# Seven 128x128 block products for P4 as well in layer 1, with stores issued ahead of loads

## The chip, the cores and the metric

The kernel runs on one core of one Trainium2 chip. The metric is the device time of one execution in microseconds (us), the median of several. A single execution of one core has a state of fast or unknown; every profiled run used here was fast, at a mean granted TensorE clock of 0.998 or 0.999 over its span. TensorE is called PE, the VectorE DVE, the ScalarE ACT, the GpSimd POOL, and SyncE SP, as in the profile.

## The reference

There are 128 graphs of 128 nodes with 512 features, and two layers of attention with 8 heads over an adjacency matrix. Everything is f32.

```python
# layer 0                                     # layer 1, on the output of layer 0
Q, K, V = x @ W_q + b_q, ...                  q, k, v = x @ Wq.T + bq, ...
scores = Q K^T / 8 + a_i + c_j + b_g          logits = q k^T / 8
       + log(adj + 1e-9)                             + log(clip(adj, 1e-8))
out = softmax(scores) V + x                   out = (softmax(logits) v) @ Wo.T + bo
                                              return layer_norm(x + out) * gamma + beta
```

Each layer has 512x512 weight matrices (three in layer 0, four in layer 1), and they take most of PE's time.

## The kernel before

Graphs are handled in groups of four: groups 0 to 31 are layer 0, groups 32 to 63 layer 1. One "matrix" is one weight applied to one group: v, q, k, and in layer 1 also o, the output matrix, which lags one group behind. There are 64 x 3 + 31 = 223 of them; the last group's output is computed plainly. The exponential of the log of the adjacency is a multiplication, so the softmax is `exp(scores) * adj`, divided by its sum, and the sum comes out of the mixing by a column of ones in v.

Each matrix is multiplied by Strassen's scheme, in the form with few additions: seven products P1 to P7 of 256x256 quarters in place of eight. A table of slots says which product stands where; "b" belongs to the matrix before. One of the seven, P2, is itself done by seven products of 128x128 blocks, in four phases "P2.1" to "P2.4" between which DVE combines what stands in PSUM:

```python
    SLOTS = ("P1", "P2.1"), ("P4 b",), ("P3 b", "P2.2"), ("P6", "P2.3"), ("P5",), ("P7", "P2.4"), ()
    PHASES = {"1": ("P1", "P2", "P5"), "2": ("P6",), "3": ("P7",), "4": ("P4", "P3")}
```

Every matmul is issued as two of 64 columns each, which run side by side on PE:

```python
        for half in HALVES:                     # columns 0 to 63, then 64 to 127
            nc.tensor.matmul(dst[half], lhsT[:, half], rhs, start=start, stop=stop, ...)
```

The rest of a group hangs on these slots: `pre` runs before a slot's products, `post` after them.

```python
            put(pre, a + 4 + step * k, scores, t, k)           # two graphs at a time, k = 0, 1
            put(pre, a + 7 + step * k, mix, t, (2 * k, 2 * k + 1))
            put(post, a + 7 + step * k, normalise, t, k)
            put(post, a + 8 + step * k, move, t, k, ...)       # o -> aT, transposed by 16 transfers
            ...
            put(post, first + (-1 if t == 0 else 2 + 7 * (b // 2) * late), load_graph, n, b, nc.sync)
            put(post, first + (11, 16 if t == NG + 1 else 13)[late], load_adjacency, n, nc.sync)
            ...
                    put(post, o + stored, store, t, k)         # h -> out, on the same queue (SP)
```

`move` transposes the attention's output into the buffer aT by sixteen transfers of 32 rows; the first eight fill columns 0 to 63 of every graph, the last eight columns 64 to 127:

```python
        for i in range(Q):
            for q in range(Q):
                src = v[i * S : (i + 1) * S, :, q // 2, (q % 2) * S : (q % 2 + 1) * S]
                engines[(i * Q + q) % len(engines)].dma_start(d[q * S : (q + 1) * S, :, i], src)
```

## Time and profile before

| | before |
|---|---|
| time, median of 3 runs (lowest to highest) | 3219.67 us (3216.62 to 3220.31) |
| profiled run | 3217.19 us, span 3215.3 us |
| busy over the span: PE, DVE, POOL | 99%, 62%, 57% |
| one group of layer 1 (scores to scores) | 55.56 us, some up to 56.7 |
| chain that ended last | PE 93%, SP's queue 3%, DMA 1% |

PE carries the time, but 3% of the chain runs through the queue that issues loads and stores. This is PE's timeline of the kernel before, in a layer 1 group (columns: start us, length us, engine, line, what, out<-in, rows and columns of the weight tile, size, count):

```profile
2231.44 1.90 PE L128 MATMUL p0o<-wo,T_o 128*64 128x256 f32 x16
2233.17 1.90 PE L128 MATMUL p2o<-wo,aT 128*64 128x256 f32 x16
2234.89 0.39 PE L128 MATMUL p1v<-wv1i,inner 128*64 128x128 f32 x4
2235.11 1.90 PE L128 MATMUL p3v<-wv,T 128*64 128x256 f32 x16
...
2237.16 2.06 PE L128 MATMUL s<-qT,kT 64*128 64x128 f32 x32
```

Products follow each other at their pitch. Between the block products of v and P3 of o (`p2o<-wo,aT`, 16 records) stands P4 of o (`p0o<-wo,T_o`), 1.73 us of work. The mixing isn't here: it ended at 2229.06.

### The profile page before, as it was taken

To read this page: it belongs to the slowest core of one execution; us is meant where nothing else is said; L and a number is where in the kernel's file an instruction comes from. 1 tells how busy PE (TensorE), PEld (TensorE's weight loads), DVE (VectorE), ACT (ScalarE), POOL (GpSimd) and SP (SyncE) were. 2 spreads that over 40 slices of the span, in tenths; PEclk is the share of its full clock that TensorE was granted. 3 is DMA by queue.
4 is the path that set the end of the run, shared out by engine and by line. 5 is a ranking of instruction groups with operands and counts; after the bars stand their busy time and mean duration, and the time that the engine had idled before them with its cause. 6 is when DMAs were issued, how large, how long until landed. Compare 5 with 4: busy or idle time off the path is not lost.

```text
span 3215.3 us, 95438 instructions
## 1 busy us (share of the span) xinstructions
PE 3192.1 (99%) x39970; PEld 2371.2 (74%) x39970; DVE 1988.4 (62%) x4075; ACT 1132.9 (35%) x1949; POOL 1826.5 (57%) x1892
## 2 busy tenths in 40 slices
PE   9999999999999999999999999999999999999998
PEld 6777777777777777777777777777777777777775
DVE  6666666666666666675565555555565555555565
ACT  2333333333333333333333333333333333333332
POOL 4434433434433434475766767676766767676775
PEclk9999999999999999999999999999999999999999
DMA  5333333333333333342434334343433334343432
GB/s 126 84 80 83 78 83 70 83 80 84 79 84 67 84 82 83 92 112 55 93 72 78 89 75 94 72 98 67 91 75 77 89 75 95 72 99 66 90 75 76
DMA packets 1017246, 265.83 MB, mean 83 GB/s; under 512 B 942704, under 2 KB 949872, under 8 KB 1016816
## 3 DMA queue, kind: packets, MB, share of 16 engines
q1 hardware_dynamic: 1015728, 258.39, 36.0%
q8 instruction: 319, 5.23, 0.7%
q10 hardware_dynamic: 832, 1.05, 0.1%
q14 instruction: 111, 0.91, 0.1%
q0 software_dynamic: 256, 0.26, 0.0%
HBM read 159.92 MB, written 67.11 MB: 71 GB/s over the span
## 4 chain that ended last, share of the span: by engine, by line
PE 93%; SPq 3%; DMA 1%; POOL 1%; DVE 1%; issue 1%; ACT 0%; DVEq 0%; POOLq 0%; ACTq 0%
PE p3v L128 10%; PE p0q L128 9%; PE p3k L128 9%; PE s L128 8%; PE av L128 7%; PE p2v L128 7%; PE p2q L128 7%; PE p2k L128 6%; PE p0o L128 6%; PE p0k L128 4%; PE p3q L128 4%; PE p0v L128 3%; SPq L128 3%; PE p2o L128 3%; PE p1q L128 3%; PE p1v L128 3%
## 5 line engine op out<-in xcount | busy, mean ns | idle before, releaser
L128 POOL TENSOR_TENSOR xn<-o,xn 128x512 f32<-128x512 f32 x128 | 151.1, 1201 | 661.2 <-DVE o L128 423.3
L128 DVE TENSOR_TENSOR e<-e,adjT 128x1024 f32<-128x1024 f32 x256 | 419.0, 1677 | 139.4 <-ACT e L128 139.4
L128 POOL TENSOR_TENSOR xn<-xn,row 128x512 f32<-128x512 f32 x256 | 361.7, 1435 | 169.9 <-DVE gw L128 138.0
L128 PE MATMUL p0q<-T,wq 128*64 128x256 f32 x2256 | 267.5, 379 | 0.0
L128 PE MATMUL p3k<-T,wk 128*64 128x256 f32 x2256 | 267.5, 379 | 0.0
L128 PE MATMUL p3v<-wv,T 128*64 128x256 f32 x2256 | 267.4, 379 | 0.0
L128 PE MATMUL s<-qT,kT 64*128 64x128 f32 x4096 | 263.1, 278 | 0.0
L128 PE MATMUL av<-v,e 128*64 128x65 f32 x8192 | 262.0, 221 | 0.0
L128 PEld LDWEIGHTS av<-v,e 128*64 128x64 f32 x8192 | 257.8, 137 | 1.0 <-issue 0.8
L128 PEld LDWEIGHTS s<-qT,kT 64*128 64x128 f32 x4096 | 238.6, 188 | 22.6 <-issue 12.1
L128 POOL TENSOR_TENSOR h<-h,gamma 128x512 f32<-128x512 f32 x122 | 156.3, 1281 | 115.0 <-ACT h L128 115.0
L128 PEld LDWEIGHTS p3k<-T,wk 128*64 128x64 f32 x2256 | 159.5, 137 | 67.4
L128 PEld LDWEIGHTS p3v<-wv,T 128*64 128x64 f32 x2256 | 159.0, 137 | 67.6
L128 PEld LDWEIGHTS p0q<-T,wq 128*64 128x64 f32 x2256 | 159.4, 137 | 67.1
L128 POOL TENSOR_TENSOR T<-xT 128x512 f32<-128x512 f32 x128 | 193.9, 1515 | 18.0 <-DVE xT L128 14.4
L128 ACT COPY o<-av 128x520 f32<-128x520 f32 x256 | 151.8, 593 | 133.2 <-PE av L128 120.8
L128 POOL TENSOR_TENSOR h<-h,xn 128x512 f32<-128x512 f32 x124 | 157.7, 1303 | 43.2 <-ACT h L128 40.4
L128 DVE SCALAR_TENSOR_TENSOR gw<-xn,gw 128x512 f32<-128x512 f32 x256 | 177.4, 693 | 4.4
L128 DVE STREAM_TRANSPOSE xT<-xT 128x512 f32<-128x512 f32 x252 | 177.1, 703 | 0.7 <-issue 0.7
L128 PE MATMUL p0o<-wo,T_o 128*64 128x256 f32 x1488 | 176.6, 379 | 0.0
L128 DVE TENSOR_TENSOR t1q<-p1q,t1q 128x128 f32<-128x128 f32 x189 | 54.5, 288 | 180.2 <-PE p1q L128 180.2
L128 POOL TENSOR_TENSOR h<-h,beta 128x512 f32<-128x512 f32 x122 | 156.5, 1283 | 9.6
(231 smaller groups left out, 6559.1 us busy)
## 6 DMA issues: line engine op xcount, KB each, us to landing
x1d<-xn SPq DMA_DIRECT2D x64, 512.0 KB, 3.0
xT<-x1d SPq DMA_DIRECT2D x512, 64.0 KB, 2.5
xn<-x1d SPq DMA_DIRECT2D x64, 512.0 KB, 6.9
xT<-in_x_dram SPq DMA_DIRECT2D x496, 64.0 KB, 2.8
xn<-in_x_dram SPq DMA_DIRECT2D x62, 512.0 KB, 4.1
aT<-o SPq DMA_DIRECT2D x984, 32.0 KB, 2.0
out_dram<-h SPq DMA_DIRECT2D x60, 512.0 KB, 4.6
adjT<-in_adj_dram SPq DMA_DIRECT2D x256, 64.0 KB, 3.7
```

Of the source, the lines that this page charges most:

```text
L128: return lambda *args, **kw: self.tc.keep_in_program_order(f(*args, **kw))
```

## The change

P4 of the layer 1 matrices is done by seven 128x128 block products too, in phases "P4.1" to "P4.4" between the outer products. That removes one block product in eight. To pay for it in the other engines, counts and small sums go to POOL; loads are issued later, so that the stores of h stand ahead of them in SP's queue; the last group's operations are reordered. Because P4 leaves slot 1, the first scores and the first mixing of a layer 1 group move one slot later (`L * (1 - k)`).

```diff
-    SLOTS = ("P1", "P2.1"), ("P4 b",), ("P3 b", "P2.2"), ("P6", "P2.3"), ("P5",), ("P7", "P2.4"), ()
+    SLOTS = (
+        ("P1", "P4.1 b", "P2.1"), ("P4 b",), ("P3 b", "P4.2 b", "P2.2"), ("P6", "P4.3 b", "P2.3"), ("P5", "P4.4 b"),
+        ("P7", "P2.4"), (),
+    )
+    INSIDE = {t: ("P2", "P4") if t > NG else ("P2",) if t else () for t in range(LAST)}
+    INSIDE.update({("qk", NG): (), ("o", NG): ()})
+    INSIDE.update({("o", t): ("P2", "P4") if t > NG else () for t in range(NG, LAST)})
...
-    for i in range(4):
-        nc.tensor.matmul(busy[:, 0:N], ones, ones, start=True, stop=True)
+    for i in range(20):
+        nc.tensor.matmul(busy[0 : P // 2, 0 : P // 2], ones, ones, start=True, stop=True)
...
-            put(pre, a + 4 + step * k, scores, t, k)
+            put(pre, a + 4 + L * (1 - k) + step * k, scores, t, k)
...
-                put(pre, a + 7 + step * k, mix, t, (2 * k, 2 * k + 1))
-                put(post, a + 7 + step * k, normalise, t, k)
+                m = a + 7 + L * (1 - k) + step * k
+                put(pre, m, mix, t, (2 * k, 2 * k + 1))
+                put(post, m, normalise, t, k)
...
-                put(post, first + (-1 if t == 0 else 2 + 7 * (b // 2) * late), load_graph, n, b, nc.sync)
+                put(post, first + (-1 if t == 0 else 2 + (8 if t > NG + 1 else 11) * (b // 2) * late), load_graph, n, b, nc.sync)
-            put(post, first + (11, 16 if t == NG + 1 else 13)[late], load_adjacency, n, nc.sync)
+            put(post, first + (11, 16 if t == NG + 1 else 14)[late], load_adjacency, n, nc.sync)
+            if "P4" in INSIDE[n]:
+                put(post, first + (18, 24)[late], lambda n: inner_sums(TS[n], n, "P4"), n)
... (phases of P4 in inner(); counts on POOL; residual, statistics and scaling of h at other slots;
     weight sums of P4; the list of the last group in another order, stores on two queues)
```

## The prediction

> **What bounds the kernel now.** I began with the page's busy times and slices.
>
> ```profile
> span 3215.3 us, 95438 instructions
> PE 3192.1 (99%) x39970; PEld 2371.2 (74%) x39970; DVE 1988.4 (62%) x4075; ACT 1132.9 (35%) x1949; POOL 1826.5 (57%) x1892
> ...
> PE   9999999999999999999999999999999999999998
> ```
>
> TensorE (PE) is busy from start to end. But the ends of matmuls are modelled and neighbours overlap, so 99% may hide waits. I therefore read the pitch, start to start, from the timeline of PE in layer 1 (columns: start us, length us, what):
>
> ```profile
> 2200.84 0.39 PE L128 MATMUL p1q<-inner,wq 128*64 128x128 f32 x4
> 2201.05 0.39 PE L128 MATMUL p1q<-xT,wq1i 128*64 128x128 f32 x4
> 2201.27 1.90 PE L128 MATMUL p3k<-xT,wk 128*64 128x256 f32 x16
> 2203.00 0.61 PE L128 MATMUL p1k<-xT,wk 128*64 128x128 f32 x8
> 2203.44 0.39 PE L128 MATMUL p1k<-inner,wk1i 128*64 128x128 f32 x4
> 2203.65 1.90 PE L128 MATMUL p0q<-T,wq 128*64 128x256 f32 x16
> ```
>
> A whole outer product (16 records: 2 output blocks x 2 k x 2 halves, each recorded twice in f32) takes 2203.00 - 2201.27 = 1.73 us, or 0.108 us a record. Eight records of 128 columns take 2203.44 - 2203.00 = 0.44 us, and four take 0.21 to 0.22 us: 0.054 us a record. The pitch is proportional to the columns, with no fixed cost to be seen, and the groups follow each other without a hole. Multiplying each form's records by its pitch gives 21,472 x 0.108 + 6,132 x 0.054 + 4,096 x 0.062 (scores, 1.99 us for 32) + 8,192 x 0.032 (mixing, about 2.0 us for 64) = about 3,166 us of 3,215. The rest is the start, the tail, changes between forms, and few waits. These are PE's waits:
>
> ```profile
> engine line waited for: us in total, times, longest us
> PE good_total L128 <- DVE good_sum L128: 5.2, 1, 5.2
> PE tr_o L128 <- ACT aT_last L128: 1.8, 2, 1.1
> ...
> PE p1o L128 <- DVE kT L128: 1.0, 1, 1.0
> PE p1o L128 <- DVE h L128: 1.0, 3, 0.3
> PE p1o L128 <- POOL T_o L128: 1.0, 1, 1.0
> ```
>
> The first two lie in the last group, the rest in layer 1, around the buffer h and at its first output matrix. So the kernel is bound by PE's stream; every matmul removed is worth its pitch as long as no other engine becomes late. How late they can be, I read from the busy times in one group of four graphs of layer 1:
>
> ```profile
> core 0: us, PE busy (x) PEld busy (x) DVE busy (x) ACT busy (x) POOL busy (x), PEclk, DMA share, GB/s
> 2200.00:2255.60 55.60, 55.60 (x692) 41.37 (x690) 32.43 (x64) 19.97 (x34) 39.29 (x42) 1.00 0.39 83
> ```
>
> DVE is 58% busy there and POOL 71%.
>
> **What the Trainium skill says.** "TensorE: Matmul & The Clock Gate", section "Back-to-back issue gap", gives about 81 ns per matmul at N=128 in a stream with weight loads, more than its N/2.4 + 2.5 formula. If 128 columns carried such a floor, smaller blocks would not pay. The trace disagrees for this form (64-column halves in pairs): 54 against 108 ns, exactly half. "TensorEngine Tiling (Array Packing)", section "PSUM Bottleneck", warns that tiling speeds up TensorE but not the reading of PSUM; this trace agrees in kind: one inner product of 0.65 us of PE is followed by two DVE operations of 0.29 us. "PSUM — Partial Sum Buffer", section "PSUM bank collisions raise a hardware error", asks for guards by bank, not by address: so each inner phase must wait until DVE has finished reading the bank of the phase before, though its columns differ. The trace before shows no run without that guard.
>
> **The change part by part.**
> (1) P4 by seven blocks. Removed: one outer product, 16 x 0.108 = 1.725 us. Added: 7 x 4 = 28 records of 128 columns, 28 x 0.0539 = 1.509 us. Gain 0.216 us a matrix (one record group of four: 8 block products become 7). It applies to groups 33 to 63 (31 x v, q, k = 93) and output matrices 33 to 62 (30): 123 x 0.216 = **-26.6 us**, all on PE's path.
> (2) q and k of group 32 lose their inner P2: 2 x 0.216 = **+0.4 us**.
> (3) DVE pays for (1): per matrix three accumulations of 0.288, two of 0.292 and one of 0.426 us, 1.87 us (2.02 for o, which splits the last): 7.6 us a group. The counts leave it (0.17 + 0.19 + 0.08 = 0.45). DVE: 32.4 + 7.6 - 0.45 = 39.6 of 54.7 us, 72%. ACT loses the plain copy of P4 (2 x 0.59 + 4 x 0.47 = 3.1 us a group).
> (4) POOL gets two sets of four 128x128 sums (8 x 0.459 = 3.7 us) and three count operations (about 0.25 each, an estimate from the 128x2 row, 0.23): 39.3 + 4.4 = 43.7 of 54.7 us, 80%.
> (5) Order. Stores of h go ahead of loads and later stages of the normalisation are spread, so h should be free earlier. Of the waits for h, kT and T_o in the loop (about 5 us of holes between starts, more than the 3.0 us listed, as modelled ends cover part of a hole) I credit 4: **-4 us**.
> (6) Last group. PE's last product ends at 3202.2, DVE's last operation at 3209.3. The chain of the last graph needs add 0.69 + statistics 0.69 + 0.18 + POOL 0.83 + 0.57 + two finishing operations 1.5 + hand-overs 0.3 = 4.7 us when DVE takes it first; it now stands behind counts and other graphs. 7.1 - 4.7 = 2.4: **-2.5 us** with stores on two queues. The longer warm-up I count as nothing.
> (7) New waits, the term I trust least. P2.2 used to follow P2.1 after two outer products, 3.45 us; now after one and a phase, 1.94 us. I placed the DVE operations of a steady group by hand in program order at their durations. Most phases fit: in k, P4.1, P2.1 of o, each two operations, are done about 0.8 us after their matmuls, with 1.1 us to spare. Two places don't. (a) The scores of the first half now start right behind phase P4.4 of k, which writes the second half of kT: PE end to DVE 0.2 + 0.43 us, against 0.5 us of scores that need only the first half, 0.1 to 0.2 us of wait. (b) The weighting by adjacency occupies DVE 2.7 to 4.1 us (longer beside POOL); behind it stand P2.4's two reads, and the next P2.1 wants the same bank: 0 to 0.4 us. A middle of 0.25 us in each of 31 groups: **+8 us**.
> Sum: -26.6 + 0.4 - 4 - 2.5 + 8 = -24.7 us. 3219.7 - 24.7 = 3195.
>
> **The rivals.**
> DVE becomes late: a phase waits for DVE each matrix. For it: 72% busy, [...]operations of 1.2 to 2 us in front of phases worth 0.2 us. Against it: DVE's idle time now is nearly all waiting for PE (the t1 groups wait 100 to 180 us for p1). At 0.2 us in every one of 123 matrices, 25 us, the gain of (1) is gone: 3,212.
> POOL becomes late: 80% busy, sums T of the next group late, and [...]DVE slows as well (weighting 2.69 us in one place, 4.12 beside POOL's sums). For it: the T_o wait above; against it: the sums are due about 13 us after their transposes. At 0.5 us a group, +15 us: 3,210.
> No new wait at all, and the old ones gone: 3219.7 - 26.2 - 5.4 - 4 = 3,184.
> A fixed cost per small matmul (the skill's 81 ns): 28 x 0.081 = 2.27 us against 1.73, +0.54 x 123 = +67 us: 3,286. The measured pitch makes this very unlikely.
>
> **Range and chances.** Part (1) is arithmetic on a measured pitch and nearly certain; (7) spans 0 to 25 us, (5) and (6) 0 to -9 together. That gives 3,183 to 3,210 for eight in ten. 2% is 64 us: faster would need more than twice the PE work removed; slower would need 90 us of new waits.
>
> **What would show it.** PE records: 39,970 + 123 x 12 - 24 + 32 (warm-up) = 41,454. P4's product on banks p0 and p3 falls by 16 records a matrix and 28 of 128 columns appear, still at 0.054. A steady layer 1 group shrinks from 55.6 to about 55.0 us (54.74 without new waits); a layer 0 group stays at 43.7. DVE about 72%, POOL about 80% in layer 1. Where (7) is real, PE waits stand at s behind DVE kT, and at p1v behind DVE h. The tail from the last product to the last DVE operation is under 5 us. The prediction is wrong if a layer 1 group takes over 55.6 us, or if the small matmuls' pitch rises.

## The result, and the profile after

| | before | after |
|---|---|---|
| median of the runs taken side by side (lowest to highest, runs) | 3219.8 us (3216.62 to 3220.31, 6) | 3202.72 us (3201.36 to 3203.58, 6) |
| ratio of the fast runs, 95% interval | | 0.9949, 0.9936 to 0.9961 |
| span of the profiled run | 3215.3 us | 3199.6 us |

The change is worth 17.1 us by the medians, half a per cent. A ratio here and below is the mean time of one kernel's fast runs over that of the other's in the same rounds, so it isn't quite the ratio of the medians quoted beside it. The predicted 3195 us was 7.7 us too low and its range of 3183 to 3210 holds the result.

These are the head of the page of the kernel after, its row of busy tenths, and its chain:

```profile
span 3199.6 us, 99332 instructions
PE 3178.8 (99%) x41454; PEld 2454.4 (77%) x41454; DVE 2165.9 (68%) x4643; ACT 1043.3 (33%) x1763; POOL 2018.3 (63%) x2337
...
PE   9999999999999999999999999999999999999998
...
PE 98%; DVE 1%; POOL 0%; DMA 0%; issue 0%; ACT 0%; SPq 0%; DVEq 0%; POOLq 0%
```

PE's records are 41,454, to the record what was predicted. The chain no longer runs through SP's queue (before: 3%). PE still reads 99%, as it did, and so says nothing about where the missing 7.7 us are.

The waits of PE in the kernel after (columns: who waited for whom, us in total, times, longest):

```profile
engine line waited for: us in total, times, longest us
PE p3v L135 <- DVE u3v L135: 2.5, 1, 2.5
PE av L135 <- DVE e L135: 1.5, 2, 1.1
```

The list of before had small waits for h, kT and T_o in layer 1; they are gone. Both waits shown are new, and both stand at group 32, on the way from layer 0 to layer 1. No wait of the steady groups is listed. Yet the starts of the scores in two neighbouring groups of the trace are 2052.36 and 2107.46, so a group takes 55.10 us. It was 55.56, and four matrices with 0.216 us less work each should make it 54.70 (55.56 - 0.86). So 0.4 us a group are lost in something that the view of waits doesn't name. The busy times of that group:

```profile
core 0: us, PE busy (x) PEld busy (x) DVE busy (x) ACT busy (x) POOL busy (x), PEclk, DMA share, GB/s
2052.36:2107.46 55.10, 55.10 (x739) 44.17 (x737) 37.81 (x86) 17.23 (x28) 43.53 (x53) 1.00 0.40 83
```

DVE is busy 37.8 of 55.1 us, 69% (predicted 72%), and POOL 43.5, 79% (predicted 80%). The loss shows only in the timeline of PE, at the place where the timeline of before was shown:

```profile
2059.60 2.04 PE L135 MATMUL av<-v,e 128*64 128x65 f32 x64
2061.46 2.01 PE L135 MATMUL p2o<-wo,aT 128*64 128x256 f32 x15
2063.19 0.38 PE L135 MATMUL p0o<-woi,innerP_o 128*64 128x128 f32 x2
2063.31 0.38 PE L135 MATMUL p2o<-wo,aT 128*64 128x256 f32 x1
...
2063.63 0.38 PE L135 MATMUL p3v<-wv,T 128*64 128x256 f32 x1
...
2066.22 2.06 PE L135 MATMUL s<-qT,kT 64*128 64x128 f32 x32
```

The mixing (`av`) now stands right in front of P3 of o. P3 is cut up: 15 of its 16 records are followed by two of the next product, then comes the sixteenth, then pieces of three products in alternation. That is what it looks like when one 64-column half runs ahead and the other lags. It goes on until the scores at 2066.22, which need both.

The time between the two profiled runs splits as follows, by the starts of matmuls in the two traces. The move of the first scores by one slot, 2.16 us (P5 and a phase, 16 records at 0.108 and 8 at 0.054), is taken out of the third and fifth line.

| stretch | before, us | after, us | difference |
|---|---|---|---|
| start to the first scores | 52.2 | 51.1 | -1.1 |
| scores of group 0 to 31 (layer 0) | 1355.1 | 1355.2 | +0.1 |
| scores of group 31 to 33 | 90.9 | 95.1 - 2.16 | +2.0 |
| scores of group 33 to 63, thirty groups | 1670.3 | 1653.8 | -16.5 |
| last scores to the end | 46.7 | 44.4 + 2.16 | -0.2 |
| sum | 3215.3 | 3199.6 | -15.7 |

Less work in thirty groups is 30 x 4 x 0.216 = 25.9 us, and 3.9 us of old waits went (shown by b2_loads below). So 25.9 + 3.9 - 16.5 = 13.3 us of new loss stand in the steady groups. The experiments look for it.

### The profile page after: what moved, and what is told of

The parts are those of the page before. It is cut to its first block, busy times and chain, and to the rows that moved or that the text cites.

```text
span 3199.6 us, 99332 instructions
## 1 busy us (share of the span) xinstructions
PE 3178.8 (99%) x41454; PEld 2454.4 (77%) x41454; DVE 2165.9 (68%) x4643; ACT 1043.3 (33%) x1763; POOL 2018.3 (63%) x2337
## 4 chain that ended last, share of the span: by engine, by line
PE 98%; DVE 1%; POOL 0%; DMA 0%; issue 0%; ACT 0%; SPq 0%; DVEq 0%; POOLq 0%
PE p3v L135 10%; PE p3k L135 10%; PE p0q L135 10%; PE s L135 8%; PE av L135 7%; PE p2v L135 7%; PE p2q L135 7%; PE p2k L135 7%; PE p0o L135 7%; PE p0k L135 4%; PE p0v L135 4%; PE p3q L135 4%; PE p2o L135 3%; PE p1v L135 3%; PE p1k L135 3%; PE p1q L135 3%
## 5 line engine op out<-in xcount | busy, mean ns | idle before, releaser
L135 PE MATMUL p3v<-wv,T 128*64 128x256 f32 (+1 forms) x2132 | 249.7, 361 | 2.5 <-DVE u3v L135 2.5
L135 PE MATMUL p3k<-T,wk 128*64 128x256 f32 (+1 forms) x2132 | 239.7, 360 | 0.0
L135 PE MATMUL p0q<-T,wq 128*64 128x256 f32 (+1 forms) x2132 | 239.7, 360 | 0.0
L135 DVE SCALAR_TENSOR_TENSOR gw<-xn,gw 128x512 f32<-128x512 f32 x256 | 196.5, 767 | 4.4
L135 POOL TENSOR_TENSOR h<-h,gamma 128x512 f32<-128x512 f32 x121 | 181.4, 1499 | 27.9 <-ACT h L135 27.9
L135 PEld LDWEIGHTS p3k<-T,wk 128*64 128x64 f32 x2132 | 149.0, 137 | 57.8
L135 PEld LDWEIGHTS p0q<-T,wq 128*64 128x64 f32 x2132 | 148.6, 137 | 58.1
L135 ACT ACTIVATE e<-s 128x1024 f32<-128x1024 f32 x128 | 124.3, 1023 | 124.9 <-PE s L135 124.9
L135 PE MATMUL p0o<-wo,T_o 128*64 128x256 f32 (+1 forms) x1368 | 161.1, 353 | 0.8 <-DVE u3o L135 0.4
```

Of the source, the lines that this page charges most:

```text
L135: return lambda *args, **kw: self.tc.keep_in_program_order(f(*args, **kw))
```

## The experiments

The kernel before ran in every call; its medians were 3220.34, 3221.34, 3222.44 and 3222.76 us (7 to 9 runs each, 3216.42 to 3225.39 in all). Ratios are against it. The calls ran on four different chips, so a difference of a microsecond or two between runs of different calls says little.

| run | base | median (range), us | ratio, 95% interval |
|---|---|---|---|
| a1_halves | after | 3191.44 (3190.85 to 3192.77) | 0.9911, 0.9898 to 0.9925 |
| a2_mixlater | after | 3210.34 (3210.00 to 3210.85) | 0.9971, 0.9955 to 0.9986 |
| b1_mixnext | before | 3225.45 (3223.32 to 3226.85) | 1.0015, 1.0000 to 1.0030 |
| a3_noP4 (wrong result) | after | 3227.29 (3225.30 to 3228.33) | 1.0023, 1.0009 to 1.0037 |
| a5_noP4 | after | 3212.41 (3212.31 to 3213.36) | 0.9975, 0.9961 to 0.9989 |
| c1_step7 | a1 | 3193.91 (3193.03 to 3196.13) | 0.9917, 0.9902 to 0.9932 |
| c2_rows | a1 | 3190.30 (3188.91 to 3191.34) | 0.9906, 0.9891 to 0.9921 |
| c4_warm | a1 | 3193.22 (3192.08 to 3193.45) | 0.9913, 0.9898 to 0.9928 |
| b2_loads | before | 3211.71 (3211.53 to 3212.54) | 0.9969, 0.9956 to 0.9983 |
| d1_step6 | c2 | 3190.08 (3189.82 to 3191.39) | 0.9903, 0.9887 to 0.9918 |
| d2_tail | c2 | 3192.30 (3191.26 to 3192.67) | 0.9908, 0.9893 to 0.9923 |
| e1_onlyP3o | after | 3192.24 (3191.40 to 3193.68) | 0.9905, 0.9888 to 0.9921 |

### The suspicion, from the built order

The built program's order on PE, with the semaphores that each matmul waits for, has this at P3 of o, the same in before and after (kept short, numbers of buffers left out):

```
p2o<-wo,aT 64x256 [waits DMAHW4,DMAHW3,DMAHW5,DMAHW2,DMAHW6,DMAHW1,DMAHW7,DMAHW0,DVE]
p2o<-wo,aT 64x256 [waits DMAHW4,DMAHW5,DMAHW3,DMAHW6,DMAHW2,DMAHW7,DMAHW1,DMAHW0]
```

The sixteen transfers of `move` go round eight queue semaphores twice. The matmul on the lower columns waits for the first eight, the one on the upper columns for the last eight. The Trainium skill, "Perfetto Trace Analysis", section "Identifying Dependency Chains", says that "instructions waiting on multiple engines may have EventSemaphore instructions inserted prior to the instruction with additional wait conditions". The traces agree: eight EVENT_SEMAPHORE instructions stand in PE's stream for these two matmuls, four for each. Their starts, read from the records of the traces themselves (us):

```
before  2231.24 .35 .46 .56 .69 .80 .90 2232.01   P3 of o starts 2233.17   (behind 16 records of 0.108)
after   2060.90 .01 .12 .22 .35 .46 .56 2061.67   P3 of o starts 2061.46   (behind 64 records of 0.029)
```

They come every 0.106 us wherever they stand, in before as well, where PE was busy with P4. The transfers had landed: in the trace of after, none of the eight queue semaphores rises between 2052.29 and 2065.80. So the waits cost only their own issue: 8 x 0.106 = 0.85 us of PE's sequencer. In before the first of them was issued 1.93 us ahead of P3, in after 0.56 us ahead. Counted in matmul records that is the same lead: 18 records start between the first wait instruction and P3 in both kernels (1.93 / 0.108 = 18; 0.56 / 0.029 = 19 by the mean pitch). That is how far PE's sequencer ran ahead there. In before, 0.85 us fit under the lead. In after they don't: the lower half of P3 starts at 2061.46, between the wait instructions, and the upper half only at 2061.77, 0.31 us later and 0.10 us after the last wait instruction.

The rival is the prediction's own account, that DVE is late at the phases.

### a1_halves: the upper half first

```diff
-        for half in HALVES:
+        for half in HALVES[::-1]:
```

> The changed kernel, but every pair of 64-column halves is issued upper half first. Theory W (waits of PE's sequencer): in the changed kernel P3 of the output matrix stands right behind the mixing, and eight semaphore-wait instructions of about 0.106 us each stand in front of its first two matmuls; the short matmuls of the mixing give PE too little queued work to hide 0.85 us, so each group of layer 1 loses about 0.33 us. The upper half waits for the later transfers, so the lower half needs no wait of its own: four wait instructions (0.42 us) stay, which the queue hides. W expects a layer 1 group of 54.7 to 54.8 us instead of 55.09, and 3191 to 3195 us in all. Rival D (my prediction's reason: DVE comes late with the inner phases): the work of DVE is the same, so 55.09 and 3202 us.

The upper columns' list asks for the second round of the same semaphores, which includes the first round, so the lower half has nothing to wait for and four instructions fall away. Measured: 3191.44 us, 11.3 less than after; a steady group takes 54.77 us (scores at 2051.22 and 2105.99), where 54.70 is the work. DVE's work is the same in kind and amount. So DVE wasn't what a group waited for. Turning every pair removes 244 of PE's semaphore instructions in all.

### a2_mixlater: the mixing two slots later

```diff
-                m = a + 7 + L * (1 - k) + step * k
+                m = a + 7 + L * (1 - k) + step * k + 2 * (t > NG and k == 0)
```

> The changed kernel, but the mixing of the first half of each group (layer 1, after group 32) two slots later, behind P3 of the output matrix and before P6 of v. W: the eight waits then stand behind 24 matmuls of 128 columns (0.054 us each), which hide them or nearly: group 54.7 to 54.85 us, 3191 to 3197 us. D: the normalisation moves closer to the next weighting, DVE is later if anything: 55.1 us or more, 3202 us or more.

Measured: 3210.34 us, 7.6 us more than after, 55.4 us a group. The theory's 3191 to 3197 us was missed, and the number of the rival D came. P3 is no longer behind the mixing, but moving the mixing, with the normalisation and the transfers behind it, brought DVE's work into another order, and now DVE is late. From PE's waits of this run, and from its timeline:

```profile
PE p1v L135 <- DVE v L135: 4.0, 23, 0.3
...
2063.27 2.16 PE L135 MATMUL p2o<-wo,aT 128*64 128x256 f32 x16
2065.21 0.44 PE L135 MATMUL p0o<-woi,innerP_o 128*64 128x128 f32 x4
2065.82 0.44 PE L135 MATMUL p1v<-wv1i,innerP 128*64 128x128 f32 x4 [0.17 <-DVE v L135]
```

The first line is new: 23 waits for v, 4.0 us. That is less than half of the 9.4 us by which the thirty groups are longer than in after (1663.2 against 1653.8), because modelled ends cover part of each hole: start to start the one shown is 0.34 us longer than the pitch. The wait list isn't hidden either. P3 takes 2.16 us instead of 1.90, and its upper half starts at 2063.52, 0.25 us behind the lower one and again 0.10 us after the last wait instruction (2063.42). The first of them was issued only 0.69 us, 12 records, ahead of P3, so the lead of 18 isn't a constant. As a test of the wait list this run failed, because the edit moved several things. It does show that DVE has little to spare at these phases, which the prediction's places (a) and (b) rested on; that in the kernel after the mixing itself (1.9 us of PE without work for DVE's phases) gives DVE its room is argued from the order, not shown.

### b1_mixnext: the loss in the kernel before, without any change to P4

```diff
-                put(pre, a + 7 + step * k, mix, t, (2 * k, 2 * k + 1))
-                put(post, a + 7 + step * k, normalise, t, k)
+                m = a + 7 + step * k + 2 * (t > NG and k == 0)
+                put(pre, m, mix, t, (2 * k, 2 * k + 1))
+                put(post, m, normalise, t, k)
...
-                    put(post, a + 8 + step * k, move, t, k, ...)
+                    put(post, m + 1, move, t, k, ...)
```

> The kernel before (no inner P4), but with the mixing of the first half moved right in front of P3 of the output matrix, where the change puts it. W: the waits that P4's product hid are exposed without any extra DVE work: group 55.56 becomes about 55.9 us, the whole 3228 to 3232 us. D: DVE has time to spare in this kernel, so no change: 55.56 and 3219 to 3221 us.

The mixing is put right in front of P3 of o, in before. Measured: 3225.45 us, 5.1 more by the medians of the call; a steady group takes 55.9 us (scores at 2115.64 and 2171.53), 0.33 more than before. PE's timeline at that place:

```profile
2125.68 2.04 PE L128 MATMUL av<-v,e 128*64 128x65 f32 x64
2127.54 2.01 PE L128 MATMUL p2o<-wo,aT 128*64 128x256 f32 x15
2129.27 0.38 PE L128 MATMUL p1v<-wv1i,inner 128*64 128x128 f32 x2
2129.39 0.38 PE L128 MATMUL p2o<-wo,aT 128*64 128x256 f32 x1
```

The same picture as in the kernel after: 15 records, two of the next product, then the sixteenth. Here DVE has nothing to do with it: between 2124.85 and 2129.80 it waits for PE. The wait instructions again stand at 0.106 us from 2126.98 to 2127.75, P3 starts at 2127.54, 18 records after the first of them, and its upper half at 2127.85, 0.10 us after the last. So mixing next to P3 makes the loss without P4's blocks. The whole stayed below the 3228 to 3232 us expected, and its interval begins at 1.0000: this run lacks most of the stores' delays of the kernel before (b2_loads below; 0.7 us of waits for a store here against 43.7 there), which offsets part of the 0.33 us a group. The group's period and the timeline are the evidence here, not the total.

### e1_onlyP3o: the turned half in this one product alone

```diff
-        for half in HALVES:
+        for half in HALVES[::turned]:        # turned is 1 unless given
...
-            product(i, t["W"], t["B"], p, side, i in ("P1", "P5"))
+            product(i, t["W"], t["B"], p, side, i in ("P1", "P5"), -1 if name[0] == "o" and i == "P3" else 1)
```

> The kernel after with the upper 64 columns first in one product alone, P3 of the output matrices of layer 1 (31 of its 253 kinds of outer products); every other matmul keeps its order. The built order shows that only this product's second list of eight queue semaphores falls away. Theory (the second list of wait instructions in PE's queue sets one half back): the whole gain of the run with all halves turned returns, 3191 to 3194 us, and a steady layer 1 group takes 54.8 us. Rival (turning the halves of all matmuls helped somewhere else, at the scores or in the phases, where the halves follow each other in another order): 3199 to 3203 us and 55.1 us a group, as the kernel after.

(The count of kinds in that text is loose: it is one product in 31 of the 223 matrices.) Measured: 3192.24 us, and the timeline of PE at the place is whole again:

```profile
2058.70 2.04 PE L135 MATMUL av<-v,e 128*64 128x65 f32 x64
2060.57 1.90 PE L135 MATMUL p2o<-wo,aT 128*64 128x256 f32 x16
2062.30 0.39 PE L135 MATMUL p0o<-woi,innerP_o 128*64 128x128 f32 x4
...
2065.00 2.06 PE L135 MATMUL s<-qT,kT 64*128 64x128 f32 x32
```

A group takes 54.77 us (scores at 2051.47 and 2106.24). The page's first line of this run says how little was taken away:

```profile
span 3191.1 us, 99212 instructions
```

The kernel after has 99332: 120 instructions less, four in each of thirty groups, and the records show that all 120 are PE's semaphore instructions (1429 against 1549). They carried 1653.8 - 1643.9 = 9.9 us over the thirty groups. The rival, that turning the halves helped elsewhere, falls: in a1_halves, with 244 such instructions fewer, the thirty groups take 1644.1 us, no less than here, so the other 124 had cost nothing where they stood. Note that P1 of o waits for the same two lists; it stands behind a product of 0.108 us records and loses nothing.

### a3_noP4 and a5_noP4: the change without P4's blocks

```diff
-    INSIDE = {t: ("P2", "P4") if t > NG else ("P2",) if t else () for t in range(LAST)}
+    INSIDE = {t: ("P2",) if t else () for t in range(LAST)}
-    INSIDE.update({("o", t): ("P2", "P4") if t > NG else () for t in range(NG, LAST)})
+    INSIDE.update({("o", t): ("P2",) if t > NG else () for t in range(NG, LAST)})
...
-                if t > NG:
-                    put(post, turned, lambda t: inner_sums(TO[t], f"o{t}", "P4"), t)
```

> The changed kernel with the inner products of P4 taken out again (P2 alone stays), everything else of the change kept: order, counts, POOL, last group. W: P4's plain product stands again between mixing and P3 and hides the waits, so a group takes 55.5 to 55.6 us; with the start 1 us shorter and the odd waits for h gone, 3215 to 3220 us, and the inner P4 itself is worth about 15 us net, not 26.6. D: with the extra 7.6 us of DVE work gone, also near 55.56; but if the new order costs something itself, a group above 55.6 us.

a3_noP4 is a failed experiment. Its result is wrong (relative error 0.62), because I left in the sums of P4's weight blocks, which alter the quarter in place that the whole P4 then reads. Its time, 3227.29 us, still tells one thing: with scores and mixing where the change puts them, but P4.1 not standing in front of P2.1, a group takes 55.94 us, and PE's waits list 23 at P2.1 of v (3.6 us). This suggests that the new slots are only good together with the new phases. a5_noP4 does it right: without those sums, and with scores and mixing back at their slots of before.

> The changed kernel without inner P4, done right: the weights' inner sums for P4 are left out too (the earlier run multiplied by altered weights), and scores and mixing stand at their slots of the kernel before, so that no later score position is mixed in. Everything else of the change stays. Expected: a layer 1 group of 55.56 us as before, without the odd longer ones (3.5 us in all gone), start 1.1 us shorter, tail as before: 3215 to 3218 us. Then inner P4 with its order is worth 13 to 15 us of the change and all the rest 2 to 4 us. If the rest alone gave 8 us or more, my account of the terms is wrong.

Measured: 3212.41 us, a ratio of 0.9975, and 55.56 us a group. I expected less gain from the rest of the change and had written that 8 us or more would put my account of it in doubt; it is 8.9 us by the medians of the call, though only 4.7 between the spans of the profiled runs (3215.3 and 3210.6). b2_loads below explains it. From here to the kernel after it is 9.7 us by medians, and to a1_halves 21.0, of 26.2 predicted for P4's blocks.

### c1_step7, c2_rows, c4_warm: the transition and the start, on top of a1

```diff
-        step = 5 if t == NG else 7                                        # c1_step7
+        step = 7
-        put(post, V2 + (10, 10, 13, 13)[c], weigh_rows, c)                # c2_rows
+        put(post, V2 + (12, 12, 13, 13)[c], weigh_rows, c)
-    for i in range(20):                                                   # c4_warm
+    for i in range(4):
```

> Upper half first, and in group 32 the second half's scores and mixing at the same distance as in every other group. In the changed kernel their weighting (4.4 us of DVE) stands in front of a phase of P4 of v in group 33 and PE waits 2.5 us, after which its clock may fall for a while. If DVE's order there is the cause, this wait goes: 2 to 4 us less than the run with the halves alone, 3187 to 3190 us. Rival: the output matrix of group 32 then waits for its moves instead, and nothing is won: 3191 us or more.

> Upper half first, and the first half of the weighted rows for the output bias (2 x 2.4 us of DVE beside POOL) behind the weighting of group 31 instead of in front of it. In the changed kernel the mixing waits for that weighting twice, 1.3 + 0.6 us; this should go: 1 to 2 us less than the halves alone, 3189 to 3191 us; 3191.4 if DVE is late there for another reason.

> Upper half first, but four warm-up matmuls instead of twenty, so that PE idles again before its first transposes. If the longer warm-up is what shortens the start, the first scores come 1 us later again (52.1 instead of 51.1 us) and the whole takes 3192 to 3193 us. If not, 51.1 and 3191.4.

The wait of 2.5 us for u3v at group 32 stands behind a weighting of e on DVE that takes 4.4 us beside POOL's sums. In c1_step7 it shrinks to 0.2, but PE's list has another in its place:

```profile
PE p1o L135 <- DVE kT L135: 3.7, 1, 3.7
```

So c1 gains nothing (3193.91 us): the wait has moved. c2_rows moves two DVE operations of the output bias away and loses the two waits for e (1.5 us), not the one for u3v; 3190.30 us is 1.1 less than a1_halves by medians of two calls, hardly more than the scatter of each. c4_warm has the 4 warm-up matmuls of before and its first scores come 51.3 us after the start, against 51.1 in a1 and after and 52.2 in before; b2_loads, with before's own start, has 51.9, and the other runs with the long warm-up have 51.2 to 52.3. The start scatters by as much as the difference, so whether the longer warm-up does anything stays open.

The transition has another cost. This is a window of a1_halves (columns: window, its length, busy us of PE, PEld, DVE, ACT and POOL with counts in brackets, granted PE clock, DMA share, GB/s):

```profile
1472.50:1477.00 4.50, 4.40 (x40) 3.23 (x42) 1.31 (x6) 0.54 (x1) 4.29 (x4) 0.64 0.31 50
```

After the wait the clock was granted at 0.64 on the mean of these 4.5 us, and 40 records ran. In c2_rows, where the wait of 2.5 us at the same product ended 1.6 us earlier, the same window held 96 (and the clock was 1.00 right behind its wait too):

```profile
1472.50:1477.00 4.50, 4.50 (x96) 4.06 (x93) 0.51 (x2) 1.18 (x2) 2.65 (x2) 1.00 0.31 53
```

In e1_onlyP3o and c4_warm the same window shows 0.62, in the kernel after and a2_mixlater 1.00; d2_tail, whose wait ended at 1471.14, has 0.62 from 1471.0 to 1475.5. It costs about 1.6 us: from the scores of group 31 to those of 33 it is 96.7 us in a1_halves and 95.1 in after, 94.8 in d2_tail and 93.1 in c2_rows. So single traces of these versions may differ by that much whatever the edit does. The Trainium skill, "TensorE: Matmul & The Clock Gate", section "What's actually happening", has the clock gate watch windows of 3413 ns that run free, so that the phase decides. This agrees in kind: the same wait of 2.5 us drops the clock in some runs and not in others. No trace shows the windows, so that their phase is the reason is not shown here.

### b2_loads: the order of loads and stores alone, in the kernel before

```diff
-                ... 2 + 7 * (b // 2) * late), load_graph, n, b, nc.sync)
+                ... 2 + (8 if t > NG + 1 else 11) * (b // 2) * late), load_graph, n, b, nc.sync)
-            put(post, first + (11, 16 if t == NG + 1 else 13)[late], load_adjacency, n, nc.sync)
+            put(post, first + (11, 16 if t == NG + 1 else 14)[late], load_adjacency, n, nc.sync)
```

> The kernel before with one part of the change alone: the loads of the second half of the next group one slot later, and those of the adjacency too, so that the stores of h are issued ahead of them. The run without inner P4 was 8.9 us faster than before by medians, but only 4.7 us by the two profiled runs; and the kernel before scatters by 7 us from run to run, that one by 1 us. Theory: output matrices wait for h until its store has landed, by a time that differs from run to run; the profiled run of before is a lucky one. Then this run scatters by 1 to 3 us only, its groups of layer 1 all take 55.56 us, and its median is 3213 to 3217 us. Rival: the 8.9 us lie in the last group or the start: then 3219 us or more, with the scatter of before.

Measured: 3211.71 us, a ratio of 0.9969, more gain than the 3213 to 3217 us expected, and every one of the thirty groups takes 55.56 us, but for the first with 55.13. In before some reached 56.7. The reason is in the waits of DVE in the kernel before:

```profile
DVE h L128 <- DMA out_dram<-h: 43.7, 24, 3.6
```

The next group's h can't be written before its store has read the buffer: 43.7 us of waiting in 24 places. Most of it lay beside PE's work; 3.9 us in the thirty groups came through. In b2_loads this line is gone. The chain of before, then the chain of b2_loads:

```profile
PE 93%; SPq 3%; DMA 1%; POOL 1%; DVE 1%; issue 1%; ACT 0%; DVEq 0%; POOLq 0%; ACTq 0%
```

```profile
PE 98%; DVE 0%; SPq 0%; DMA 0%; POOL 0%; issue 0%; ACT 0%; DVEq 0%; ACTq 0%; POOLq 0%
```

SP's queue falls from 3% to 0. The runs of before scatter over 3 to 7 us in a call, those of b2 over 1.0 us, and the profiled run of before (3217.19 us) is one of its fastest: that is why spans give 5.5 us (3215.3 to 3209.8) and medians 10.7. The loss in before differs from run to run, and the single trace shows a small case of it; the other runs of before were not traced, so this is read from their scatter. It accounts for a5_noP4 to within 0.7 us: 3212.41 against 3211.71 us.

### d1_step6 and d2_tail: two tries for a better version

```diff
-        step = 5 if t == NG else 7                                                 # d1_step6, on c2
+        step = 6 if t == NG else 7
-        (13, begin_one, u, 3), ... (14, finish_one, u, 3),                         # d2_tail, on c2
+        (12, scale, u, 3), (13, store_one, u, 3),
```

> Upper half first, rows for the bias later, and in group 32 the second half's scores and mixing one slot later (between the kernel changed and the distance of the other groups, which made the output matrix wait 3.7 us). If the two waits trade against each other, the sum stays 2 to 4 us: 3189 to 3191 us. If one slot frees the phase of P4 and the moves still land in time, 3186 to 3188 us.

> Upper half first, rows for the bias later, and in the last group one more graph of the group before is finished by ScalarE and POOL instead of two operations of 0.75 us on DVE. After the last product DVE is busy without a gap for 6.3 us; if that run of operations sets the end, it ends 1.5 us earlier: 3188 to 3189.5 us. If POOL's share delays the last graph's statistics instead: 3190 us or more.

d1_step6 took 3190.08 us against 3190.30 of c2_rows: its wait for u3v fell to 0.3 us and two others of 1.3 us each came. d2_tail, which takes one graph's normalisation off DVE in the tail and gives it to ACT and POOL, took 3192.30 us: no gain. Its tail was 1.2 us longer, and the 1.7 us of the lower clock above are in its profiled run as well. Both are misses. c2_rows and d1_step6 are the fastest versions, some 12 us below the kernel after; the turned half in one product gives nearly all of that.

## Why the prediction was right or wrong

The time fell inside the range, 7.7 us above the middle. By its steps, in the spans of the profiled runs:

| step | predicted, us | measured, us |
|---|---|---|
| (1), (2) fewer records | -26.2 | the work is gone as counted; 54.77 of 54.70 us a group in e1 |
| (5) waits for h, kT, T_o | -4 | -3.9 in the thirty groups and -1.2 in groups 31 to 33 (where kT stood), -5.5 in all (b2's span), -10.7 by medians |
| (6) tail | -2.5 | -0.2 |
| (7) new waits | +8 | +13.3 in thirty groups, 9.9 of it the wait list |
| transition to layer 1 | not there | +2 |
| start | 0 | -1.1, within its scatter |

**(1) and (2) were right.** The record count is exact, and 128-column records still follow at 0.054 us: in the timeline of after, `p1v<-wv,xT` with 8 records starts at 2058.94 and the next product 0.44 us later. The rival of a fixed cost per small matmul is dead. Two readings behind it were off, without harm to the term. The skill's 81 ns were set against 54 ns, but 54 is a mean over two halves that run side by side; a pair of 128-column records comes every 108 ns, which a floor of 81 wouldn't touch, so what kills the rival is that the pitch stays proportional to the columns. And 64 records of mixing take 1.87 us from start to start (0.029 each), not 2.0, so the stream adds up to about 3,145 us and not 3,166.

**(3) and (4) were right within a few per cent.** DVE 69% and POOL 79% of a group.

**(5) was right in the trace and too small in the medians.** The step that was off is "I credit 4": I took it from one profiled run, which was a fast one. b2_loads gives 10.7 us by medians for the same edit.

**(6) failed.** The step was "it now stands behind counts and other graphs", which assumed two finishing operations behind the last graph's statistics. This is the end of the kernel after, from the timeline of all engines (columns as above, "x2" two operations in one line):

```profile
3185.57 1.02 PE L135 MATMUL po<-wo_plain,aT_last 128*128 128x512 f32 x2
...
3187.18 0.68 DVE L135 TENSOR_TENSOR h_last<-po,xn 128x512 f32<-128x512 f32 x1
...
3188.73 1.38 DVE L135 SCALAR_TENSOR_TENSOR h_last<-h_last,rs,beta 128x512 f32<-128x512 f32 x2
...
3190.69 0.74 DVE L135 SCALAR_TENSOR_TENSOR h_last<-h_last,mv,gamma 128x512 f32<-128x512 f32 x1
...
3191.35 0.74 DVE L135 SCALAR_TENSOR_TENSOR h_last<-h_last,rs,beta 128x512 f32<-128x512 f32 x1
...
3192.74 0.73 DVE L135 SCALAR_TENSOR_TENSOR h<-h,rs,beta 128x512 f32<-128x512 f32 x1
```

After the last product (2 of its records, end 3186.59) come the add at 3187.18 and the statistics, and then six finishing operations and one begin, 0.66 us apart and without a hole until 3193.47. That is 6.9 us where 7.1 were before and 4.7 predicted. I counted two finishing operations, 1.5 us; seven such operations were queued, and DVE ran them one after the other.

**(7) was right to be there and wrong in its cause.** "Two places don't [fit]", it said, the first scores behind P4.4 of k and P2.1 behind the weighting, both DVE. No listed wait of PE stands there in the kernel after, and what it said would show the term, "PE waits stand at s behind DVE kT, and at p1v behind DVE h", isn't there. What the runs showed in its place is PE's own wait instructions: b1_mixnext makes the loss without P4's blocks and e1_onlyP3o removes it with 120 instructions fewer. The size was near (0.25 us predicted a group, 0.44 measured), which was luck. The other 3.4 us, 0.11 a group, I did not follow up; their cause stays open. The idea itself wasn't empty: a2_mixlater, with DVE's work in another order, has DVE waits of the kind that it foresaw, and at group 32 a phase of P4 does wait behind a weighting, the 2.5 us for u3v.

**The transition was missing.** I treated group 32 as two matrices without inner P2. Two new waits there cost 4.0 us (1.5 and 2.5), while before had about 1.6 (kT 1.0, t1q 0.6); a lower clock may follow, as three later runs show, though not in the trace of the kernel after.

Of the rivals, "DVE becomes late" with 0.2 us in every matrix did not come, nor "POOL becomes late": POOL is 79% busy, but PE's list has no wait behind it in the steady groups, and the old one for T_o is gone. "No new wait at all", 3184 us, remains out of reach of the best version by 6 us; the 5.4 us in its sum are not worked out in the prediction.

## What to carry to other kernels

A matmul that waited for many semaphores cost PE's sequencer 0.106 us for every instruction inserted for it, even when all were long satisfied. That is free while the sequencer is far enough ahead (1.93 us of long records hid 0.85 us of waits) and shows where it is not (0.56 us of short ones did not). So put long records in front of such a matmul, or order the reads so that the first waits for everything and the second for nothing. When an engine reads 99% busy and no wait is listed, compare the period of a steady group with its work, and look for products that are cut into pieces in the timeline. A gain that is credited from one trace should be checked against the scatter of the other runs: where a kernel's runs scatter more than its neighbour's, the trace may be a good case of a wait that is usually larger.

## What the Trainium skill lacked or had wrong

- "Perfetto Trace Analysis", section "Identifying Dependency Chains", names the inserted EventSemaphore instructions but no cost. Here each took 0.106 us of PE's issue though already satisfied, and eight of them behind 64 short matmuls set one 64-column half back by 0.31 us; the view of waits shows nothing of it.
- No page has how far PE's sequencer runs ahead of the matmuls in a running kernel, in time or in records ("TensorE: Matmul & The Clock Gate" has only the depth of PE's queue). Here 18 matmul records started between the first wait instruction and P3 in before, after, b1_mixnext and e1_onlyP3o (1.93 us of records of 0.108 us, 0.56 us of records of 0.029 us), and 12 in a2_mixlater (0.69 us).
- "TensorE: Matmul & The Clock Gate", section "Back-to-back issue gap", gives about 81 ns at N=128 with weight loads, and no figure for two 64-column halves side by side in f32. Here such a pair of records came every 108 ns, 54 ns a record on the mean, so the page's figure is not tested.
- "TensorE: Matmul & The Clock Gate", section "What's actually happening", has an idle window of about 3.4 us before the clock falls. Here a listed wait of 2.5 us was enough in a1_halves, c4_warm, e1_onlyP3o and d2_tail (granted clock 0.62 to 0.64 on the mean of the 4.5 us behind it), and not in the kernel after, a2_mixlater and c2_rows (1.00).
